# A fused attention and mixture-of-experts kernel: two score tiles of the second head pair issued ahead of the last three products of the first, and the seventh batch's scatters one at a time

## The chip, the cores and the metric

One core of one Trainium2 chip. The metric is device microseconds of one execution of the whole program, measured by repeated runs; the figure that a forecast stands on is the median of the runs. A profile is one further execution, taken with the hardware profiler.

## What is computed

The input is x of 8 batches (B) x 1024 tokens (S) x 512 features (D), float32. Two layers follow each other, each with a layer norm ahead of it and the input added behind it.

```python
# attention layer, 16 heads of 32 features; xh = layernorm(x) cut into heads
theta_q = xh / (1.0 + jnp.abs(w_q)) + b_q + t * phi_q
theta_k = xh / (1.0 + jnp.abs(w_k)) + b_k + t * phi_k
theta_v = xh / (1.0 + jnp.abs(w_v)) + b_v
Q = jnp.concatenate([cos_q, sin_q], axis=-1)      # 64 wide
K = jnp.concatenate([cos_k, sin_k], axis=-1)
...
# mixture of experts: 8 experts, the best 2 for each token, at most 160 rows for each batch and expert
probs = jax.nn.softmax(x @ Wr + br, axis=-1)
topk_p, topk_e = jax.lax.top_k(probs, K)
...
h = jax.nn.relu(jnp.einsum('enc,ech->enh', buf, W1) + b1[:, None, :])
y = jnp.einsum('enh,ehc->enc', h, W2) + b2[:, None, :]
```

Scores are Q K^T with a causal mask and a softmax; the values are cosine plus sine of theta_v, and the attention's output goes through a sine and a cosine once more before the input is added. In the second layer a token's place in the queue of its expert decides whether it is kept.

## The kernel before

**The loop.** The attention is one loop of 32 iterations n, `for n in range(NCK)`. Iteration n is batch b = n // 4 and chunk c = n % 4: four heads, 128 features, all 1024 tokens. The four heads are two pairs (0 and 1). A pair's keys lie as 64 features by 1024 tokens on each half of the partitions, so each step issues two matmuls, one for each head, on half of the array each. Queries are taken in two halves h of 512.

**Scores.** `scores(pair, h, es)` is a generator: each step makes one tile of exponentials. It takes a PSUM tile from `two_banks()` (a pool of three such tiles, shared by everything that uses it), issues the score matmuls (L685), for blocks on the diagonal the mask as further matmuls (L699), and one exponential on ScalarE from PSUM to SBUF (L705). For h = 0 there are three steps (512 queries wide, 512 made of two pieces, 256 wide), for h = 1 seven.

**Products.** `attend(n, pr, h, es, halves)` has the same three or seven steps: a step multiplies one tile of exponentials by the values into one PSUM bank `av` (L719). With the last step of a half goes one instruction on VectorE, which takes the bank to SBUF with a scaling, `av_sb` (L727).

**turn.** `turn(pr, halves, p)` transposes a pair's two `av_sb` tiles into a `two_banks()` tile by 16 transposes on TensorE (L215), the first eight from queries 0 to 511, the last eight from 512 to 1023; VectorE then takes a reciprocal of the softmax sums (L754) and multiplies (L756).

**Order of an iteration.** `some(count, *gens)` steps generators. In iteration n TensorE sees, in this order: scores of pair 0 (with products of the iteration before in between), seven products left from the iteration before (three, four), turn(1) of the iteration before, then the products of pair 0 (three, and after some work on VectorE and ScalarE for the next iteration's keys, the rest), then scores of pair 1, turn(0), the other score tiles, and the first products of pair 1. Between them stand steps of the router of the batch before (`route_on`), in iterations with c = 1 and c = 2: transposes, the logits (L858) and the sums (L875) of a group of tokens, with VectorE's instructions for them. `qk_post` makes the next iteration's queries and keys on VectorE (L450); its second half, `rest(post)`, stands behind turn(0).

**Who decides the order.** For TensorE, VectorE, ScalarE and SyncE the order of the program text is kept, the order is written by hand. Waits come from data and buffer dependencies.

**Scatters.** When the router has placed the 1024 x 2 rows of a batch, 16 indirect DMAs on GpSimd write pairs of token number and gate to `slot_d[b]` in HBM (L770, in `scatter`). They write one tensor, so each waits for the one before, unless `together` is given: then it is declared that their rows are their own, and they are put behind the last weight mixture on GpSimd's queue so far. `fetch_slots(b)` reads the result and waits for all 16. Batches 0 to 5 are scattered within the loop, at c = 3 of the next batch, one at a time. Batch 6 (the seventh) and batch 7 are scattered in `ending()`, together: eight of batch 6 at the first step, the other eight ahead of the router's step "tiles" of batch 7, and batch 7's sixteen at the end.

**The experts.** `ending()` is a generator whose steps are taken inside the first products of the experts: `layer1` (L1189) takes one step for each product. The first chunk's weights are mixed on GpSimd for the first six of its quarters q (`mix_w1`, L1173, four subtractions, into a pool of two buffers), and the scatters of batch 6 stand between these mixtures on GpSimd's queue. Behind `layer1` comes `layer2` (L1234).

The middle of an iteration, where the change lies, and the end of the loop are in the listing.

Of the kernel before, what the change touches and what calls it, by code (L numbers as in the profile page):

```python
# [25 lines left out]
NTT = S // P  # L26
NCH = D // P
HPC = P // DH
E, HID, TOPK = 8, 2048, 2
# [44 lines left out]
def preln_attn_moe_kernel(  # L74
# [133 lines left out]
    def two_banks():  # L208
        return ps_sc.tile([P, 2, 512], F32, name="ps_s")
# [232 lines left out]
    def square(p):  # L442
        f = p.bitcast(U16).rearrange("p (s two) -> p s two", two=2)[:, :, 0]
        nc.scalar.activation(p.bitcast(F32), f, AF.Square, bias=split_c, scale=1.0 / FINE)

    def sine(r):
        nc.scalar.activation(r.bitcast(F32), r, AF.Sin, scale=STEP_ACT)
# [196 lines left out]
    def o_pre(n, pos):  # L644
        c = n % NCH
        p = pos.bitcast(I32)
        r = trig.tile([P, S], I32, name="t_r")
        nc.vector.tensor_tensor(by_token(p), by_token(pos), along(bias_o, c), ALU.add)
        angle(p, r)
        return p, r  # L650

    def o_post(n, st):

        f, s = st[0], st[1].bitcast(F32)
        b, ch = divmod(n, NCH)
        times(s, f, s)
        xt, stats = mid_tiles[b]
        xs = xt[:, :, ch * P : (ch + 1) * P]
        nc.vector.scalar_tensor_tensor(xs, by_token(s), SUM_UNIT, xs, ALU.mult, ALU.add)
        yield  # L660
        for t in range(NTT):
            nc.vector.bn_stats(stats[:, t, ch, :], xt[:, t, ch * P : (ch + 1) * P])


    def tiles_of(h):


        def block(kb, at=0):
            q0 = max(512 * h, kb * P)
            return kb, q0, 512 * (h + 1) - q0, at  # L670

        d = 4 * h
        full = [[block(kb)] for kb in range(d + 1)]
        return full + [[block(d + 1), block(d + 3, 3 * P)], [block(d + 2)]]

    def scores(pair, h, es):

        for parts in tiles_of(h):
            n = sum(w for _, _, w, _ in parts)
            ps = two_banks()  # L680
            own_keys = parts[0][0] >= 4 * h
            for kb, q0, w, at in parts:
                for a in range(2):
                    r = slice(a * 64, (a + 1) * 64)
                    nc.tensor.matmul(  # L685
                        ps[:, a, at : at + w], lhsT=pair[r, 1, kb * P : (kb + 1) * P],
                        rhs=pair[r, 0, q0 : q0 + w], start=at == 0, stop=not own_keys,
                        skip_group_check=True,
                    )
            if own_keys:  # L690

                for part, w in ((0, 64), (1, P)):
                    for a in range(2):
                        r = slice(a * 64, (a + 1) * 64)
                        out_, late = ps[:, a, :w], later_b[r, part, :w]
                        if len(parts) == 2:
                            out_ = ps[:, a, :].rearrange("p (k q) -> p k q", q=P)[:, ::3, :w]
                            late = late.unsqueeze(1).to_broadcast([64, 2, w])
                        nc.tensor.matmul(  # L699
                            out_, lhsT=keys_b[r, part, :], rhs=late,  # L700
                            start=False, stop=part == 1, skip_group_check=True,
                        )

            e = ep.tile([P, 2, n], F32, name=f"e_{n}", bufs=8 if n == 512 else 2)
            nc.scalar.activation(  # L705
                e, ps[:, :, :n], AF.Exp, scale=UNIT * UNIT / math.sqrt(2 * DH)
            )
            es.append(e)
            yield

    def attend(n, pr, h, es, halves):

        vt = v_tiles[n % 2]
        av = ps_av.tile([P, 512], F32, name="av")
        tiles = tiles_of(h)
        for i, parts in enumerate(tiles):
            for kb, q0, w, at in parts:
                for a in range(2):
                    nc.tensor.matmul(  # L719
                        av[a * 64 : (a + 1) * 64, q0 - 512 * h :],  # L720
                        lhsT=vt[:, kb, 2 * pr + a, :], rhs=es[i][:, a, at : at + w],
                        start=kb == 0, stop=i + 1 == len(tiles),
                    )
            if i + 1 == len(tiles):
                av_sb = avp.tile([P, 512], F32, name="av_sb")
                q = 2 * (n % NCH) + pr
                nc.vector.tensor_scalar(av_sb, av, inv_o[:, q : q + 1], None, ALU.mult)  # L727
                halves.append(av_sb)
            yield

    def some(count, *gens):

        for gen in gens:
            while count and next(gen, 0) is None:
                count -= 1
# [7 lines left out]
    def turn(pr, halves, p):  # L743

        ps = two_banks()
        for t in range(NTT):

            by_halves(
                ps[:, :, t * 64 : (t + 1) * 64],
                halves[t // 4][:, t % 4 * P : (t % 4 + 1) * P],  # L750
            )
        av = ps.rearrange("p a (t f) -> p t a f", f=64)
        rec = small.tile([P, NTT, 2, 1], F32, name="rec")
        nc.vector.reciprocal(rec, av[:, :, :, DH : DH + 1])  # L754
        dst = p.rearrange("p (t a d) -> p t a d", a=HPC, d=DH)
        nc.vector.tensor_tensor(  # L756
            dst[:, :, 2 * pr : 2 * pr + 2, :], av[:, :, :, :DH],
            rec.to_broadcast([P, NTT, 2, DH]), ALU.mult,
        )
# [3 lines left out]
    scattered = {b: [] for b in range(B)}  # L763
    mixed = []

    def scatter(count=2 * NTT * TOPK, together=False):

        for _ in range(min(count, len(scatters))):
            b, idx, src = scatters.pop(0)
            queued = nc.gpsimd.indirect_dma_start(  # L770
                out=slot_d[b], out_offset=bass.IndirectOffsetOnAxis(ap=idx, axis=0),
                in_=src, in_offset=None,
            )
            ins = queued.ins
            if together:
                tc.add_manual_dep(
                    ins, mixed[-1].name,
                    mybir.DependencyInfo(
                        mybir.DependencyClass.NoSync, mybir.DependencyReason.DATA
                    ),  # L780
                    reason="behind the mixture",
                )
                for other in scattered[b]:
                    tc.declare_no_dep(ins, other, reason="rows of their own")
            scattered[b].append(ins)
# [506 lines left out]
    def experts_begin():  # L1292
# [6 lines left out]
        mix_w1(0, 0)  # L1299

    def experts(ending):
        pools["hp"] = to_end.pool("hp", NHQ, **right)
        pools["ps_tr"] = to_end.pool("ps_tr", 2, space=PSUM, reuse_waits="tile")
# [67 lines left out]
    for n in range(NCK):  # L1371
        more, late = n + 1 < NCK, last is not None
# [14 lines left out]
        products = [attend(n, 0, h, es[h], halves[0]) for h in range(2)]  # L1387
        if late:
            products.insert(0, attend(n - 1, 1, 1, e11, halves1))
        ahead = [scores(pairs[0], h, es[h]) for h in range(2)]  # L1390
# [8 lines left out]
        def route_on(slot):  # L1399
            if c == slot and route is not None:  # L1400
                next(route)
# [61 lines left out]
        if c == 3 and b > 0:  # L1463
            next(route)
            if b > 1:
                fetch_slots(b - 2)
            if b < B - 1:
                scatter()
# [14 lines left out]
        if more:  # L1483
            post = qk_post(qk_st)
            next(post)
        some(NTT, *products)

        es, halves1 = [[], []], []
        ahead = [scores(pairs[1], h, es[h]) for h in range(2)]
        route_on(1)  # L1490
        route_on(2)
        some(2, *ahead)
        turn(0, halves[0], pos_n)
        next_pairs = rest(post) if more else None
        some(1, *ahead)
# [42 lines left out]
    def ending():  # L1538

        o_st = o_pre(NCK - 1, pos_n)  # L1540
        scatter(NTT * TOPK // 2, together=True)
        yield
        sine(o_st[1])
        square(o_st[0])
        for _ in range(3):
            yield
        for _ in o_post(NCK - 1, o_st):
            yield
        yield
        for name in router(B - 1):  # L1550
            if name == "tiles":
                scatter(together=True)

            for _ in range({"tiles": 5, "places": 5}.get(name, 1)):
                yield
        fetch_slots(B - 2)
        scatter(together=True)
        fetch_slots(B - 1)

    experts(ending())  # L1560

# [30 lines left out]
```

## Time and profile before

| | |
|---|---|
| time, median of 3 runs | 3274.17 us (3273.48 to 3274.39) |
| the profiled execution: its own time | 3271.21 us |
| its span in the profile | 3269.5 us |
| TensorE clock granted, mean | 0.997 of full speed |
| VectorE busy | 2255.6 us, 69% |
| ScalarE busy | 1323.1 us, 40% |
| GpSimd busy | 420.2 us, 13% |
| score matmuls L685, TensorE | 599.5 us in 3072 instructions |
| products L719, TensorE | 524.6 us in 3072 instructions |
| scatters L770, GpSimd | 155.6 us in 128 instructions |
| first product of the experts (L1189) | at 1274.89 us |

The span begins with the first instruction and ends with the last; the execution's own time also has what lies around it (1.7 us here). The execution that was profiled is 3.0 us under the median of the timed runs. Up to about 1275 us the attention loop runs, behind that the experts; an iteration of the loop takes 36 to 42 us. Where a row of the profile ends in brackets, the first number is the idle time of that engine just ahead, in us, and what stands behind the arrow is the work that ended it; "remote" and "issue" name no instruction. A shape such as 64*128 64x512 is that of the weights and of the moving data of a matmul. L numbers are lines of the kernel before.

### The profile page before, as it was taken

To read this page: it belongs to the slowest core of one execution; us is meant where nothing else is said; L and a number is where in the kernel's file an instruction comes from. 1 tells how busy PE (TensorE), PEld (TensorE's weight loads), DVE (VectorE), ACT (ScalarE), POOL (GpSimd) and SP (SyncE) were. 2 spreads that over 40 slices of the span, in tenths; PEclk is the share of its full clock that TensorE was granted. 3 is DMA by queue.
4 is the path that set the end of the run, shared out by engine and by line. 5 is a ranking of instruction groups with operands and counts; after the bars stand their busy time and mean duration, and the time that the engine had idled before them with its cause. 6 is when DMAs were issued, how large, how long until landed. Compare 5 with 4: busy or idle time off the path is not lost.

```text
span 3269.5 us, 48752 instructions
## 1 busy us (share of the span) xinstructions
PE 3188.8 (98%) x18942; PEld 2164.7 (66%) x18942; DVE 2255.6 (69%) x4961; ACT 1323.1 (40%) x1617; POOL 420.2 (13%) x387
## 2 busy tenths in 40 slices
PE   5999999999999998999999999999999999999998
PEld 2444444444444444688688688688688688688687
DVE  8888888878788675755755755755755755855854
ACT  7888887888887874211111111111201201201201
POOL 3000202011120212311011011011011011011010
PEclk9999999999999999999999999999999999999999
DMA  5435454453545352323223223323322322322321
GB/s 163 143 98 164 133 146 143 135 156 104 181 117 159 94 172 56 117 55 85 90 50 81 91 52 77 94 52 71 100 50 73 101 47 73 103 46 71 104 42 26
DMA packets 235254, 319.74 MB, mean 98 GB/s; under 512 B 22456, under 2 KB 155280, under 8 KB 222992
## 3 DMA queue, kind: packets, MB, share of 16 engines
q1 hardware_dynamic: 211664, 273.38, 28.5%
q0 software_dynamic: 22912, 43.22, 7.5%
q8 instruction: 150, 2.46, 0.3%
q14 instruction: 80, 0.66, 0.1%
q10 hardware_dynamic: 448, 0.02, 0.0%
HBM read 187.62 MB, written 61.82 MB: 76 GB/s over the span
## 4 chain that ended last, share of the span: by engine, by line
PE 57%; DVE 0%; DMA 0%; issue 0%; POOL 0%; POOLq 0%; DVEq 0%
PE ps_p L1234 29%; PE ps_p L1189 27%; PE ps_t L1135 1%; DMA out_dram<-y,slots 0%; DMA slots<-slot_d 0%; DVE w_t L1068 0%; DVE w L1067 0%; DVE w_t L1066 0%; DVE w_t L1069 0%; POOL slot_d L770 0%; POOLq L1588 0%; POOL slots L1005 0%; DVE y L1250 0%; DVE p L1271 0%; DVE p L1272 0%
## 5 line engine op out<-in xcount | busy, mean ns | idle before, releaser
L705 ACT ACTIVATE e<-ps_s 128x1024 f32<-128x1024 f32 (+1 forms) x640 | 569.6, 937 | 195.5 <-PE ps_s L685 111.9
L685 PE MATMUL ps_s<-qk 64*128 64x512 f32 (+3 forms) x3072 | 599.5, 506 | 39.4 <-DMA qk<-qk_r 12.4
L1234 PE MATMUL ps_p<-w,hid 128*128 128x256 f32 x2560 | 567.2, 379 | 0.0
L1234 PEld LDWEIGHTS ps_p<-w,hid 128*128 128x128 f32 x2560 | 484.4, 190 | 66.7 <-DVE u L1210 0.3
L719 PE MATMUL av<-e,v 128*64 128x512 f32 (+3 forms) x3072 | 524.6, 491 | 0.6 <-ACT e L705 0.6
L1234 PE MATMUL ps_p<-w_t,hid 128*128 128x256 f32 x1920 | 430.3, 379 | 0.6 <-DVE w_t L1068 0.6
L685 PEld LDWEIGHTS ps_s<-qk 64*128 64x128 f32 x3072 | 262.1, 188 | 228.4 <-issue 106.6
L1234 PEld LDWEIGHTS ps_p<-w_t,hid 128*128 128x128 f32 x1920 | 361.3, 190 | 48.2 <-DVE w_t L1068 1.0
L719 PEld LDWEIGHTS av<-e,v 128*64 128x64 f32 x3072 | 200.5, 137 | 285.7 <-issue 267.7
L1189 PE MATMUL ps_p<-xe,w 128*128 128x256 f32 (+1 forms) x1024 | 297.8, 434 | 1.1 <-issue 1.1
L1189 PE MATMUL ps_p<-xe,t 128*128 128x256 f32 (+1 forms) x1024 | 297.0, 433 | 0.0
L1189 PE MATMUL ps_p<-xe_s,t 128*128 128x256 f32 (+1 forms) x1024 | 296.9, 433 | 0.0
L770 POOL DMA_INDIRECT slot_d<-token,slot x128 | 155.6, 1215 | 975.6 <-issue 621.2
L1265 ACT COPY p<-ps_p 128x256 f32<-128x256 f32 x40 | 14.7, 369 | 604.8 <-PE ps_p L1234 604.8
L1189 PEld LDWEIGHTS ps_p<-xe,t 128*128 128x128 f32 x1024 | 194.3, 190 | 81.2 <-issue 1.0
L1189 PEld LDWEIGHTS ps_p<-xe,w 128*128 128x128 f32 x1024 | 193.4, 190 | 82.1 <-DVE hid L1207 3.7
L1189 PEld LDWEIGHTS ps_p<-xe_s,t 128*128 128x128 f32 x1024 | 194.3, 190 | 80.7 <-issue 0.4
L1094 POOL DMA_INDIRECT xg<-xn_d,source x76 | 74.5, 980 | 1073.6 <-PE ps_t L1135 1064.3
L1256 POOL DMA_INDIRECT out_dram<-y,slots x80 | 126.5, 1581 | 624.3 <-DVE y L1251 624.3
L1204 ACT ACTIVATE p<-ps_p,b_t 128x256 f32<-128x256 f32 (+1 forms) x128 | 65.4, 511 | 335.6 <-PE ps_p L1189 178.4
L1221 ACT ACTIVATE hid<-hid,b_more 128x256 f32<-128x256 f32 (+1 forms) x128 | 71.8, 561 | 278.0 <-DVE hid L1220 270.7
L1208 ACT ACTIVATE hid<-hid 128x256 f32<-128x256 f32 (+1 forms) x128 | 60.1, 470 | 297.9 <-DVE hid L1207 289.8
(224 smaller groups left out, 3822.9 us busy)
## 6 DMA issues: line engine op xcount, KB each, us to landing
w<-in_L_ffn_W_dram SPq DMA_DIRECT2D x256, 256.0 KB
w<-in_L_ffn_W_dram SPq DMA_DIRECT2D x64, 512.0 KB
qk<-qk_c SPq DMA_DIRECT2D x124, 256.0 KB
qk<-qk_r SPq DMA_DIRECT2D x124, 256.0 KB
qk_base<-base_d SPq DMA_DIRECT2D x28, 1024.0 KB
xn_d<-xn SPq DMA_DIRECT2D x72, 256.0 KB
x_mid<-in_L_attn_x_dram SPq DMA_DIRECT2D x16, 1024.0 KB
out_dram<-x_mid SPq DMA_DIRECT2D x8, 2048.0 KB
```

The lines of the kernel that those rows point to most:

```text
L685: nc.tensor.matmul(ps[:, a, at : at + w], lhsT=pair[r, 1, kb * P : (kb + 1) * P], rhs=pair[r, 0, q0 : q0 + w], start=at == 0, stop=not own ...
L705: nc.scalar.activation(e, ps[:, :, :n], AF.Exp, scale=UNIT * UNIT / math.sqrt(2 * DH))
L719: nc.tensor.matmul(av[a * 64 : (a + 1) * 64, q0 - 512 * h :], lhsT=vt[:, kb, 2 * pr + a, :], rhs=es[i][:, a, at : at + w], start=kb == 0, ...
L770: queued = nc.gpsimd.indirect_dma_start(out=slot_d[b], out_offset=bass.IndirectOffsetOnAxis(ap=idx, axis=0), in_=src, in_offset=None,)
L1094: ins = nc.gpsimd.indirect_dma_start(out=xg, out_offset=None, in_=xn2_d[i % 2], in_offset=bass.IndirectOffsetOnAxis(ap=source[:, e, j0 + j ...
L1135: nc.tensor.transpose(ps[:, c, :], xg[:, c * P : (c + 1) * P], ident)
L1189: nc.tensor.matmul(ps, lhsT=weights[:, k, :], rhs=rows[:, k, :], start=k == 0, stop=k == 1)
L1204: nc.scalar.activation(p1, product(b11, a11), AF.Identity, bias=b1_t[:, e * NHC + q : e * NHC + q + 1])
L1208: nc.scalar.activation(h11, h11, AF.Relu)
L1221: nc.scalar.activation(h12, h12, AF.Relu, bias=more)
L1234: nc.tensor.matmul(ps, lhsT=hs[k][:, part, cols], rhs=ws[k][weight], start=k == 0, stop=k == NHQ - 1,)
L1256: ins = nc.gpsimd.indirect_dma_start(out=out, out_offset=bass.IndirectOffsetOnAxis(ap=meta[:, e, jj[r], 0:1], axis=0), in_=ys[r], in_offse ...
```

## The change

Two edits. In the loop, seven products of pair 0 are left at that point, those of half 1. Before, all seven are issued, then the router's steps, then pair 1's score generators are made and stepped twice, which gives the first two score tiles, and then comes turn(0). After, four of the seven are issued, then the two score tiles, then the last three products with their `av_sb`, then the router's steps, and turn(0). Iteration 0 has its products used up before this point, so that there nothing moves.

In `scatter` a third way, `late`: behind the last mixture, like `together`, but each scatter still waits for the one before on the same tensor. `ending()` scatters batch 6 in this way: eight at its first step as before, and the other eight as four and four, at the first and the fourth step of the router of batch 7, in place of eight at its step "tiles". Batch 7's sixteen stay together. In the built program GpSimd's queue thereby holds twelve scatters, the mixture of one quarter, four scatters and the next mixture, where it held eight, a mixture, eight, and a mixture.

```diff
--- before.py
+++ after.py
@@ -763,7 +763,7 @@
     scattered = {b: [] for b in range(B)}
     mixed = []
 
-    def scatter(count=2 * NTT * TOPK, together=False):
+    def scatter(count=2 * NTT * TOPK, together=False, late=False):
 
         for _ in range(min(count, len(scatters))):
             b, idx, src = scatters.pop(0)
@@ -772,7 +772,7 @@
                 in_=src, in_offset=None,
             )
             ins = queued.ins
-            if together:
+            if together or late:
                 tc.add_manual_dep(
                     ins, mixed[-1].name,
                     mybir.DependencyInfo(
@@ -780,6 +780,7 @@
                     ),
                     reason="behind the mixture",
                 )
+            if together:
                 for other in scattered[b]:
                     tc.declare_no_dep(ins, other, reason="rows of their own")
             scattered[b].append(ins)
@@ -1483,13 +1484,14 @@
         if more:
             post = qk_post(qk_st)
             next(post)
-        some(NTT, *products)
+        some(4, *products)
 
         es, halves1 = [[], []], []
         ahead = [scores(pairs[1], h, es[h]) for h in range(2)]
+        some(2, *ahead)
+        some(NTT, *products)
         route_on(1)
         route_on(2)
-        some(2, *ahead)
         turn(0, halves[0], pos_n)
         next_pairs = rest(post) if more else None
         some(1, *ahead)
@@ -1538,7 +1540,7 @@
     def ending():
 
         o_st = o_pre(NCK - 1, pos_n)
-        scatter(NTT * TOPK // 2, together=True)
+        scatter(NTT * TOPK // 2, late=True)
         yield
         sine(o_st[1])
         square(o_st[0])
@@ -1547,9 +1549,12 @@
         for _ in o_post(NCK - 1, o_st):
             yield
         yield
+        steps = 0
         for name in router(B - 1):
-            if name == "tiles":
-                scatter(together=True)
+
+            if steps in (0, 3):
+                scatter(NTT * TOPK // 4, late=True)
+            steps += 1
 
             for _ in range({"tiles": 5, "places": 5}.get(name, 1)):
                 yield
```

## Prediction

> **What bounds the kernel now.** I began with the page's busy times and slices.
>
> ```profile
> PE 3188.8 (98%) x18942; PEld 2164.7 (66%) x18942; DVE 2255.6 (69%) x4961; ACT 1323.1 (40%) x1617; POOL 420.2 (13%) x387
> PE   5999999999999998999999999999999999999998
> ```
>
> TensorE is at 98%, full from the second slice on: an edit counts only by the TensorE time or idling that it adds or takes. So I read the order of time on TensorE in one iteration of the attention loop, n=15 (c=3). Columns: start, us, engine, line, operation.
>
> ```profile
> 624.71 7.96 PE L719 MATMUL av<-e,v 128*64 128x512 f32 x48
> 632.60 1.13 PE L685 MATMUL ps_s<-qk 64*128 64x512 f32 x4
> 634.73 0.66 PE L215 MATMUL ps_s<-ident,av_sb 64*128 64x64 f32 x16
> 635.22 0.66 PE L685 MATMUL ps_s<-qk 64*128 64x256 f32 x4
> 636.01 1.99 PE L685 MATMUL ps_s<-qk 64*128 64x512 f32 x8
> 638.42 2.37 PE L719 MATMUL av<-e,v 128*64 128x512 f32 x16
> 640.73 2.85 PE L685 MATMUL ps_s<-qk 64*128 64x512 f32 x12
> ```
>
> Ten products (L719), two score tiles, the 16 transposes of turn(0), the 256-wide tile, two 512-wide tiles. There is no idle but 0.20 us ahead of 636.01, where the weight load waits for the exponential ("0.20 <-ACT e L705" in the same view). ScalarE and VectorE in that stretch:
>
> ```profile
> 632.39 1.28 ACT L705 ACT_TABLE_LOAD   x1
> 633.85 2.75 ACT L705 ACTIVATE e<-ps_s 128x1024 f32<-128x1024 f32 x3 [0.17 <-PE ps_s L699]
> 632.71 0.75 DVE L727 TENSOR_SCALAR av_sb<-av,inv_o 128x512 f32<-128x512 f32 x1 [0.59 <-PE av L719]
> ```
>
> ScalarE loses 0.17 us to the score tiles; and L727, which makes the `av_sb` that turn(0) reads, runs 632.71 to 633.46 wholly under the two score tiles. The change takes that cover away. One place has the new order already: the end of the loop, products and then a turn.
>
> ```profile
> 1266.64 5.81 PE L719 MATMUL av<-e,v 128*64 128x512 f32 x32
> 1272.38 0.46 PE L215 MATMUL ps_s<-ident,av_sb 64*128 64x64 f32 x8
> 1273.30 0.46 PE L215 MATMUL ps_s<-ident,av_sb 64*128 64x64 f32 x8 [0.46 <-DVE av_sb L727]
> 1272.50 0.75 DVE L727 TENSOR_SCALAR av_sb<-av,inv_o 128x512 f32<-128x512 f32 x1 [9.45 <-PE av L719]
> ```
>
> Eight transposes go at once (queries 0 to 511, ready long before); the other eight wait for L727. Last, the place where scatters are issued together, iteration n=31:
>
> ```profile
> 1247.52 1.13 PE L685 MATMUL ps_s<-qk 64*128 64x512 f32 x4
> 1251.19 0.70 PE L685 MATMUL ps_s<-qk 64*128 64x256 f32 x4 [0.87 <-issue]
> 1252.87 1.13 PE L685 MATMUL ps_s<-qk 64*128 64x512 f32 x4 [0.89 <-ACT e L705]
> 1257.16 1.92 PE L685 MATMUL ps_s<-qk 64*128 64x512 f32 x4 [3.17 <-DVE o_p L756]
> 1262.17 2.85 PE L685 MATMUL ps_s<-qk 64*128 64x512 f32 x12
> 1256.04 0.26 DVE L754 RECIPROCAL rec<-ps_s 128x16 f32<-128x16 f32 x1 [7.64 <-remote]
> 1244.68 0.99 POOL L770 DMA_INDIRECT slot_d<-token,slot  x1 [14.72 <-DVE token L982]
> 1253.57 0.96 POOL L770 DMA_INDIRECT slot_d<-token,slot  x1 [0.30 <-issue]
> POOL slot_d L770 <- DMA slot_d<-token,slot: 234.6, 89, 6.3
> ```
>
> L754 needs only turn(0), whose transposes are recorded from 1249.66 on, yet starts at 1256.04; an exponential due at 1252 starts at 1256.19, also "remote". Completion on TensorE is seen some 4 to 6 us late while GpSimd issues scatters back to back, and until just after. The last line counts the scatters that go one at a time (batches 0 to 5): 89 waits, none beside such a stall.
>
> **The change part by part, on TensorE's time.**
>
> *No instruction is added.* By the built order VectorE, ScalarE and SyncE keep their instructions, order and waits; TensorE changes order, GpSimd order and waits. No DMA is moved past another on SyncE.
>
> *A second block of products, iterations 1 to 30.* Count a product of 512 columns as one unit: the x48 row is 9 units in 7.89 us (624.71 to 632.60), the x16 row 2.5 in 2.31 (638.42 to 640.73). The difference gives 5.58/6.5 = 0.858 us a unit, so 0.165 us for each block as such. Going from a mask into products costs more than into a turn: 609.14 to 609.32 against 624.03 to 624.11, 0.10. Together 0.265 us.
>
> *turn(0) uncovered.* 1272.38 to 1273.30 is 0.92 us for eight transposes; all sixteen take 0.49 at 634.73, so half is 0.25: +0.67. Bounds: the idle alone, 0.46, and the whole of L727 with its 0.12 start, 0.87. I take 0.67, the same pattern. Queued behind on TensorE are the 256 tile and everything after it; on VectorE L754, L756 and the second half of the key post-processing (L450, 2.28 us) go late with it, by no more than TensorE itself.
>
> *What is won.* The scores come 2.3 us sooner, so ScalarE starts right after the table load. TensorE gains what it waited for that: 0.20 a time (bounds 0 and 0.27, 635.22 to 636.01 against 0.52 for the same tile at 623.59).
>
> - c=3 and c=0, n=3, 4, 7, ... 28: 14 times 0.265+0.67-0.20 = 0.735, 10.3 us.
> - c=1, n=5, ... 29: seven times. Now the router's matmuls (L858, L875) stand between products and turn: 557.04 to 557.74, 0.70, and cover the 0.67. 0.07 each, 0.5 us.
> - c=2, n=6, ... 30: seven times. L858 covers 596.36 to 596.72, 0.36: 0.31+0.265-0.20, and about 0.08 because VectorE's four place instructions (597.15 to 598.12) now follow the late L727 and hold the PSUM slot that the next score tile wants. 0.45 each, 3.2 us.
> - n=1, 2: no router, and no wait for ScalarE to win: 0.94 each, 1.9 us. n=0: products are used up before, nothing moves.
>
> Sum: +15.9 us. Bounds: with 0.46 for the wait and 0.27 won, +9; with 0.87 and nothing won, +25.
>
> *Scatters of batch 6 one at a time.* Now eight and eight together (1.26 us apart), then 12 and four, each waiting for the one before. The six series of batches 0 to 5 took 54 to 64 us for 15 steps, 3.9 us a step on the mean, 2.36 at the least. The stall goes: 1247.52 to 1262.17 is 14.65 us; the same stretch in n=15 is 8.13, less 0.59 for transposes that n=31 hasn't, plus this change's 0.735: 8.28. Gain 6.4 us. It includes the half clock after the idle (granted 0.72 in 1256 to 1262; the tile at 1257.16 took 1.85 us for 0.96). Bounds: 0 if the stall has another cause, 7 if the small waits at 1297 to 1302 go too.
>
> *What is queued behind them.* GpSimd's weight mixtures (L1173) for the third and fourth quarter. Twelve from 1244.68 at 3.9 end at 1291.5; the mixture's second part is then ready about 1293. TensorE wants it at 1298.17 now, 1291.8 after the gain: 1 us late at the mean step, nothing at 2.36. The stretch 1244 to 1256 has a DMA share of 0.02 against 0.39 at 476 to 536, so I take a step near 2.4 and no cost. The four others end before 1305, the fourth quarter wants its mixture at 1317.56. Unhidden, each 1 us of step costs 12.
>
> A rule that speaks against it stands in the Trainium skill, "DMA: Bandwidth & Descriptors", section on the SWDGE path: a transfer issued by GpSimd has a fixed cost of about 2 us, mostly the wait for the write to be confirmed, so waiting for each one lays that bare. By an estimate from that page twelve would take 12 x (0.96+2.0) = 35.5 us, and the sum would stay as it is.
>
> **Sum.** 15.9 - 6.4 = +9.5 us. The profiled execution took 3271.21 around a span of 3269.5; its span would be 3279.0. It is 3.0 under the median of the runs, 3274.17, on which the forecast stands: 3283.7 us. Its own range is +4 to +15: 3278 to 3289.
>
> **Rivals.**
>
> 1. *ScalarE paces the iterations, and its head start counts whole: faster.* The place is the first exponential after the table load: idle before it 0.17 at c=3 and c=0, 0.70 at c=1, 0.67 at c=2. If TensorE's later waits for ScalarE took up the 0.94, the gain would be 14 x 0.17 + 7 x 0.70 + 7 x 0.67 = 12.0, with the 6.4 of n=31 18.4: 3255.8. It decides from 0.94 us of later waiting per iteration. For it: ScalarE is at 70 to 80% here. Against: past 636.01 n=15 shows no such wait. 13%.
> 2. *The stall of n=31 stays,* being due to something else: +15.9, 3290.1. For it: "remote" names no cause. Against: the stall comes again beside the next series issued together (1363.50, 2.76 idle at ScalarE's p), never beside single ones. 15%.
> 3. *The serial scatters hold the mixtures up.* At the slowest series' step, 63.5/15 = 4.23, the third quarter is 1295.4+2.4-1291.8 = 6.0 late: +15.5, 3289.7. Against: the empty DMA queues. 8%.
> 4. *Gain and loss cancel:* the wait at its low bound, the gain at its high one: +9-7 = +2, 3276. 10%.
>
> **How the numbers follow.** Main case 54%. A run here tells no change from one under 0.2%, 6.5 us. A seventh of the main case lies under that, with rival 4 that is 17%; faster is rival 1, 13%, and 2% of surprises; slower the rest, 68%. The range 3268 to 3292 leaves out rival 1 and the ends of 2 and 3.
>
> **What would show it.** TensorE in c=3 and c=0: two score tiles inside the products, a turn in two halves of eight with about 0.46 idle for L727 (some 16 times), and no wait at the first 512 tile; no ScalarE idle after the table load. n=31: no "remote" wait, clock 1.00 there. L1189 never waiting for L1173's mixture. I am wrong if turn(0) shows no idle, if L754 in n=31 still starts 6 us late, or if an iteration of c=3 stays at 35.87 us (634.73 to 670.60) instead of 36.6.

## The result and the profile after

In the same series of runs the changed kernel took 3279.11 us (median of nine, 3274.85 to 3283.11) and the kernel before 3273.63 us (median of nine, 3269.91 to 3274.39): 5.5 us slower, a ratio of 1.0018, 95% interval 1.0010 to 1.0027. The forecast was 9.5 us, in a range of its own of +4 to +15. The two profiled executions differ by more, spans of 3279.9 and 3269.5 us, because the one of before was a short one of its kernel and the one of after a long one; the sizes below are therefore taken from single iterations and from medians, not from the two spans.

TensorE in iteration n=15 (c=3) of the changed kernel, the counterpart of the stretch shown for before; columns are start, us, engine, line, operation, and in brackets the idle ahead of it. From here on a line number in a row is that of the run's own kernel (L1190 after is L1189 before):

```profile
634.79 1.13 PE L685 MATMUL ps_s<-qk 64*128 64x512 f32 x4
...
637.02 2.37 PE L719 MATMUL av<-e,v 128*64 128x512 f32 x16
639.33 0.46 PE L215 MATMUL ps_s<-ident,av_sb 64*128 64x64 f32 x8
640.25 0.46 PE L215 MATMUL ps_s<-ident,av_sb 64*128 64x64 f32 x8 [0.46 <-DVE av_sb L727]
640.55 0.65 PE L685 MATMUL ps_s<-qk 64*128 64x256 f32 x4
...
641.12 1.94 PE L685 MATMUL ps_s<-qk 64*128 64x512 f32 x8
```

The turn is split in two halves of eight, and the second waits 0.46 us for `av_sb`. The wait of 0.20 us ahead of the first 512-wide tile, which before had at 636.01, is gone. VectorE and ScalarE in the same stretch:

```profile
639.45 0.75 DVE L727 TENSOR_SCALAR av_sb<-av,inv_o 128x512 f32<-128x512 f32 x1 [2.64 <-PE av L719]
638.04 1.94 ACT L705 ACTIVATE e<-ps_s 128x1024 f32<-128x1024 f32 x2
641.33 0.60 ACT L705 ACTIVATE e<-ps_s 128x512 f32<-128x512 f32 x1 [1.35 <-PE ps_s L215]
```

ScalarE does start its exponentials right after the table load, without the 0.17 us of before, and then stands 1.35 us for TensorE, which is in the turn. The head start is lost at once.

Iteration n=31, where before had TensorE idle for 0.87, 0.89 and 3.17 us; TensorE, VectorE and GpSimd:

```profile
1263.86 0.46 PE L215 MATMUL ps_s<-ident,av_sb 64*128 64x64 f32 x8
1264.78 0.46 PE L215 MATMUL ps_s<-ident,av_sb 64*128 64x64 f32 x8 [0.46 <-DVE av_sb L727]
...
1267.52 2.37 PE L719 MATMUL av<-e,v 128*64 128x512 f32 x16
1265.29 0.26 DVE L754 RECIPROCAL rec<-ps_s 128x16 f32<-128x16 f32 x1 [0.56 <-PE ps_s L215]
1261.05 0.97 POOL L770 DMA_INDIRECT slot_d<-token,slot  x1 [1.42 <-DMA slot_d<-token,slot]
```

The scatters go every 2.4 us or a little more (twelve from 1258.63 to 1287.01, 2.58 us a step), and L754 waits 0.56 us for the transposes, where it waited 7.64. The granted clock from 1255 to 1265 is 1.00, where it was 0.83.

The length of an iteration, from the start of the sixteenth exponential (of twenty) of the iteration before it to that of its own, is worked out from the trace. Means over n=4 to 29 without n=19, which stands by itself; us (the runs below the first two are described under Experiments):

| kernel | c=3 | c=0 | c=1 | c=2 | n=19 | n=31 |
|---|---|---|---|---|---|---|
| before | 35.87 | 35.66 | 43.75 | 37.46 | 35.87 | 45.14 |
| after | 36.59 | 36.14 | 43.82 | 38.01 | 37.96 | 38.83 |
| scores_alone | 36.59 | 36.13 | 43.81 | 38.01 | 37.96 | 45.24 |
| scatters_alone | 35.88 | 35.71 | 43.71 | 37.47 | 35.88 | 39.30 |
| one_tile_behind | 36.17 | 35.86 | 43.88 | 37.76 | 37.23 | 38.48 |
| two_in_flight | 35.88 | 35.68 | 43.58 | 37.47 | 35.87 | 40.91 |
| before_again | 35.88 | 35.59 | 43.73 | 37.47 | 35.87 | 46.57 |
| filled_again | 35.88 | 35.75 | 43.55 | 37.47 | 35.88 | 39.29 |

The iterations n=1 to n=30 together take 1160.56 us in the changed kernel and 1145.42 in before: 15.1 us more. In n=31 it takes 6.3 us less. (Single iterations of before take 35.4 to 44.1 us in these, a little more than the 36 to 42 given at the start.)

The end of the first part of the experts in the changed kernel, TensorE:

```profile
1282.54 4.51 PE L1190 MATMUL ps_p<-xe,w 128*128 128x384 f32 x8 [1.13 <-issue]
...
1370.05 1.56 PE L1190 MATMUL ps_p<-xe,t 128*128 128x384 f32 x4 [3.62 <-issue]
1371.44 1.45 PE L1190 MATMUL ps_p<-xe_s,w 128*128 128x384 f32 x4
1375.18 12.31 PE L1235 MATMUL ps_p<-w,hid 128*128 128x256 f32 x48 [2.28 <-DVE hid L1208]
```

Here batch 7's sixteen scatters are still issued together, and TensorE stands 3.62 and 2.28 us; before had one idle of 2.76 us at this place. The first row took 4.51 us, where before had 2.82 for the same eight products: the granted clock is 0.50 from 1283.12 to 1286.53. Of the 10.4 us between the two profiled spans 8.8 lie in the loop (15.1 - 6.3), 2.8 behind it, and 1.2 go the other way ahead of it. In the 2.8 are the two things seen here, 3.1 us more of idle and 1.7 of clock, and against them shorter waits of TensorE further on, told below.

### The profile page after: what moved, and what is told of

Its sections match the earlier page's. It is cut to its first block, busy times and chain, and to the rows that moved or that the text cites. A ratio compares the mean times of both kernels' runs of the same rounds, so it can differ in the third digit from the quotient of the medians.

```text
span 3279.9 us, 48776 instructions
## 1 busy us (share of the span) xinstructions
PE 3196.8 (97%) x18942; PEld 2162.3 (66%) x18942; DVE 2252.9 (69%) x4961; ACT 1319.0 (40%) x1617; POOL 418.5 (13%) x387
## 4 chain that ended last, share of the span: by engine, by line
PE 74%; DVE 4%; issue 1%; DMA 1%; ACT 1%; SPq 0%; POOLq 0%; DVEq 0%; ACTq 0%
PE ps_p L1235 29%; PE ps_p L1190 28%; PE av L719 7%; PE ps_s L685 7%; PE ps_t L1136 1%; PE ps_s L215 1%; PE ps_s L699 1%; DVE qk_f L526 0%; ACT e L705 0%; DVE qk_r L450 0%; DVE av_sb L727 0%; DMA xn_d<-xn 0%; DMA qk<-qk_r 0%; DVE xT L839 0%; DVE xn L814 0%
## 5 line engine op out<-in xcount | busy, mean ns | idle before, releaser
L1190 PE MATMUL ps_p<-xe,t 128*128 128x256 f32 (+1 forms) x1024 | 297.1, 433 | 3.6 <-issue 3.6
L1190 PE MATMUL ps_p<-xe,w 128*128 128x256 f32 (+1 forms) x1024 | 299.4, 435 | 1.1 <-issue 1.1
L1190 PE MATMUL ps_p<-xe_s,t 128*128 128x256 f32 (+1 forms) x1024 | 296.9, 433 | 0.0
L1190 PEld LDWEIGHTS ps_p<-xe,t 128*128 128x128 f32 x1024 | 194.3, 190 | 84.9 <-issue 4.6
L1190 PEld LDWEIGHTS ps_p<-xe,w 128*128 128x128 f32 x1024 | 194.1, 191 | 82.9 <-DVE hid L1208 3.7
L1190 PEld LDWEIGHTS ps_p<-xe_s,t 128*128 128x128 f32 x1024 | 194.3, 190 | 80.8 <-issue 0.7
```

What stands on the lines that cost most here:

```text
L1190: nc.tensor.matmul(ps, lhsT=weights[:, k, :], rhs=rows[:, k, :], start=k == 0, stop=k == 1)
```

## Experiments

Each series of four ran on a chip of its own, with the kernel before beside it, so that a difference between series can be one of the chip or of the hour. The median of before was 3275.6 us in the first series, 3263.9 in the second and 3274.8 in the third, so a kernel is compared only with before in its own series.

### First series: the parts, and two ways of undoing half of one

**scores_alone.** The new order of scores and products with the old scatters.

```diff
-        some(NTT, *products)
+        some(4, *products)
...
+        some(2, *ahead)
+        some(NTT, *products)
         route_on(1)
         route_on(2)
-        some(2, *ahead)
```

> The new order of score tiles and products alone; the scatters are as in the kernel before. Theory (the products' own block and the uncovered av_sb cost TensorE 0.72 us in an iteration with c=3, 0.55 with c=2): the loop gains 13 to 15 us up to n=30, the stall of n=31 stays (L754 waits over 5 us, TensorE 4 to 5 us idle), total +12 to +16 us, 3286 to 3290. Rival A (the order costs little, and the 10 us between the two profiled executions are mostly luck of the last stage): total +4 to +7. Rival B (ScalarE's head start counts): faster by over 5 us.

Measured: 3291.15 against 3275.61 us, +15.5 (ratio 1.0046, 1.0032 to 1.0060). The loop costs 15.4 us by the trace, and the stall of n=31 stays (n=31 takes 45.24 us). VectorE, then TensorE:

```profile
1266.65 0.75 DVE L727 TENSOR_SCALAR av_sb<-av,inv_o 128x512 f32<-128x512 f32 x1 [6.74 <-remote]
1267.46 0.46 PE L215 MATMUL ps_s<-ident,av_sb 64*128 64x64 f32 x8 [2.23 <-DVE av_sb L727]
1272.12 1.18 PE L685 MATMUL ps_s<-qk 64*128 64x512 f32 x4 [2.71 <-DVE o_p L756]
```

With the new order the wait is split in two: `av_sb`, which has to see the end of the last product, starts late, and TensorE stands 2.23 us for it; L754 then waits 3.59 us, less than the 5 expected. TensorE's 2.23 and 2.71 us of idle are the 4 to 5 expected. The rival of a cheap order falls, and ScalarE's pace with it.

**scatters_alone.** The old order with the new scatters.

```diff
-        scatter(NTT * TOPK // 2, together=True)
+        scatter(NTT * TOPK // 2, late=True)
...
-            if name == "tiles":
-                scatter(together=True)
+            if steps in (0, 3):
+                scatter(NTT * TOPK // 4, late=True)
+            steps += 1
```

> The scatters of batch 6 one at a time as in the changed kernel, with the old order of scores and products. Theory (scatters issued back to back make TensorE's completions late): iteration n=31 is 38.1 us instead of 45.1, first product of the experts near 1268.5, total -4 to -7 us, 3267 to 3270, unless the stall beside batch 7's sixteen scatters grows, which it may by up to 4. Rival (the stall of n=31 has another cause, and went because n=31 came at another time): n=31 keeps a wait of L754 of over 4 us, total -1 to +1.

Measured: 3266.03 against 3275.61 us, -9.6 (0.9969, 0.9959 to 0.9980). The stall of n=31 is gone, more is won than expected, and batch 7's stall stays:

```profile
1249.43 0.26 DVE L754 RECIPROCAL rec<-ps_s 128x16 f32<-128x16 f32 x1 [2.62 <-PE ps_s L215]
1355.49 1.56 PE L1190 MATMUL ps_p<-xe_s,w 128*128 128x384 f32 x4 [3.05 <-ACT p L1205]
```

Most of L754's 2.62 us is the time of the score tiles and transposes that TensorE has ahead of it. The two parts add up: +15.5 - 9.6 = +5.9, against +5.5 for both together.

**one_tile_behind.** The changed kernel with the second score tile behind the last products.

```diff
-        some(2, *ahead)
+        some(1, *ahead)
         some(NTT, *products)
         route_on(1)
         route_on(2)
+        some(1, *ahead)
```

> The changed kernel, but only the first score tile goes ahead of the last three products; the second stands behind them (and behind the router's steps), so that it covers the av_sb instruction of 0.75 us again. Theory (0.67 of the 0.735 us is the uncovered av_sb): no idle of 0.46 us in the turn, iterations with c=3 take 35.9 to 36.0 us instead of 36.59, with c=2 37.4 to 37.7 instead of 38.01, and the total is 9 to 13 us under the changed kernel's 3279.1: 3266 to 3270. Rival (it is the split into two blocks of products, or ScalarE's order, that costs): c=3 stays at 36.4 to 36.6, total 3277 to 3280.

Measured: 3272.51 us, -3.1 against before (0.9992, 0.9983 to 1.0001); c=3 takes 36.17 us, between the two theories. TensorE in n=15:

```profile
632.66 1.13 PE L685 MATMUL ps_s<-qk 64*128 64x512 f32 x4
...
633.80 2.37 PE L719 MATMUL av<-e,v 128*64 128x512 f32 x16
636.11 1.14 PE L685 MATMUL ps_s<-qk 64*128 64x384 f32 x8
...
637.24 0.66 PE L215 MATMUL ps_s<-ident,av_sb 64*128 64x64 f32 x16
```

The turn is whole again, sixteen transposes and no idle. What stays above before, 36.17 - 35.88 = 0.29, is the second block of products; and the wait for ScalarE ahead of the 512-wide tile is back (0.30 us from the mask at 638.22 to 638.52, against 0.08 in the changed kernel). My expectation of 35.9 to 36.0 had kept that gain, which one tile ahead doesn't bring. So in c=3: 0.29 for the block, 0.22 won, and 0.715 - 0.29 + 0.22 = 0.65 for the uncovered turn. The 0.65 is what is left over; read from the rows the turn takes 1.22 us (639.33 to 640.55) for 0.49 before, 0.73 more, so the split between the terms is good to some 0.1 us.

**two_in_flight.** The kernel before, with each scatter of the series issued together waiting for the one two places ahead.

```diff
-                for other in scattered[b]:
+                for other in scattered[b][:-2] + scattered[b][-1:]:
                     tc.declare_no_dep(ins, other, reason="rows of their own")
+                for other in scattered[b][-2:-1]:
+                    tc.add_manual_dep(
...
```

> The kernel before, with one thing added: in the series issued together a scatter waits for the one two places before it, so at most two are on their way, where eight could be. A single one takes 2.4 us from issue to its release, so that two at a time can still be issued every 1.3 us. Theory A (it is the dense issue on GpSimd that makes TensorE's completions late): the stall of n=31 stays, L754 waits over 5 us, total within 2 us of before. Theory B (it is the number of writes on their way): the wait of L754 is under 1.5 us, n=31 takes 38 to 39 us, the stall at batch 7's series is gone too, total -6 to -11 us.

Measured: 3279.50 us, +3.9 (1.0010, 1.0001 to 1.0019), which neither theory had. VectorE, GpSimd and TensorE:

```profile
1253.39 0.26 DVE L754 RECIPROCAL rec<-ps_s 128x16 f32<-128x16 f32 x1 [5.06 <-PE ps_s L685]
1248.95 0.96 POOL L770 DMA_INDIRECT slot_d<-token,slot  x1 [0.79 <-DMA slot_d<-token,slot]
1377.83 0.18 DVE L1093 TENSOR_SCALAR source<-slots 128x32 int32<-128x32 int32 x1 [14.49 <-DMA slots<-slot_d]
1379.33 1.22 PE L1242 MATMUL ps_p<-w_t,hid 128*128 128x256 f32 x2 [10.46 <-DVE w_t L1076]
```

Three of seven gaps between the scatters of n=31 grew from 0.30 to 0.7 or 0.8 us, and the stall shrank (n=31 40.9 us, between 39.3 and 45.1). Batch 7's stall went, but that series now took from 1335.66 to 1371.9 instead of some 20 us, VectorE waited 14.49 us for its slots with the weight mixtures queued behind, and TensorE 10.46 us for those. Dense issue and the number on their way were not told apart: the scatters of n=31 were still 1.46 us apart on the mean, and two at a time left 1.6 us of the stall (40.9 against 39.3).

### Second series: dense issue by itself, and batch 7

**filled.** The kernel before, with an instruction that no output uses behind each of the eight scatters of n=31.

```diff
+            if together and b == B - 2 and len(scattered[b]) <= NTT:
+                tc.keep_in_program_order(
+                    nc.gpsimd.tensor_tensor(spare, spare, spare, ALU.subtract)
+                )
```

> The kernel before, with an ordinary GpSimd instruction of about 1 us (a subtraction on a spare tile) behind each of the eight scatters of batch 6 in n=31. Nothing waits for the write before, up to eight may be on their way, but a scatter is issued every 2.4 to 2.8 us as in the serial series, and GpSimd is never idle. Theory A (the dense issue of scatters makes TensorE's completions late): the wait of L754 falls from 7.6 to under 2.5 us, n=31 takes 38.5 to 40 us instead of 45.1, total -4 to -7 us against before. Theory B (it needs GpSimd waiting, idle, or each write confirmed before the next): L754 still waits over 5 us, n=31 stays over 43, total within 2 us of before.

Measured: 3263.38 against 3263.93 us (1.0001, 0.9991 to 1.0010). That is theory B's total, and n=31 at 39.30 us is theory A's: on this chip it tells nothing. The trace shows why. These are the times at which TensorE's completions are recorded while sixteen scatters of batch 7 are issued back to back, in two kernels that do it alike:

```
rows_late (second series):      1332.92 1334.21 1335.50 1336.79 1338.08 1339.37 1340.66 1341.95 ...
scatters_alone (first series):  1335.57 1336.97 1342.13 1343.42 1354.77 1354.84 1354.90 1354.96 ...
```

On the second chip they come every 1.29 us, as the matmuls end. On the first there is a silence of 11.4 us, and then what was due comes 0.06 us apart, while TensorE's own rows go on ending at most 1.4 us apart: the work is not late, its report is. On the chip of the second series dense scatters hold up no completion.

**last_serial.** scatters_alone with batch 7's scatters one at a time too (`scatter(late=True)` in place of `together=True` at the end of `ending`).

> scatters_alone with batch 7's sixteen scatters one at a time too. Theory: TensorE's 3 us of idle beside that series (3.05 in scatters_alone) goes, but the fetch of the slots (L1006) comes 20 to 45 us later, and VectorE waits for it at L1086 with the mixing of the second layer's weights (L1067 to L1070) queued behind, for which TensorE waits: 8 to 30 us of idle at L1235, total +5 to +28 us against scatters_alone's 3266, 3271 to 3294. Rival (the mixing has lead enough, so that the stall's end counts): total -3 to -6 against it, 3260 to 3263.

Measured: 3287.89 us, +24.0 against before (1.0072, 1.0056 to 1.0087). VectorE, then TensorE:

```profile
1386.16 0.18 DVE L1086 TENSOR_SCALAR source<-slots 128x32 int32<-128x32 int32 x1 [28.89 <-DMA slots<-slot_d]
1387.67 1.22 PE L1235 MATMUL ps_p<-w_t,hid 128*128 128x256 f32 x2 [24.86 <-DVE w_t L1069]
```

As the theory has it: the wait moves to the one instruction on VectorE that needs the slots, and what is queued behind it stops TensorE. This is what issuing together is good for.

**rows_late** and **last_serial_rows_late.** The same two, scatters_alone and last_serial, with that instruction moved behind the mixtures.

```diff
-            if i == 0:
-                find_rows(1)
             rest(mixes)
...
-                aside = behind(2, aside)
+                aside = behind(8, aside)
             for block in range(nh):
+                if i == 0 and block == 1:
+                    find_rows(1)
```

> scatters_alone with the instruction that reads the slots (L1086) moved on VectorE from ahead of the last weight mixtures to the second block of layer2, and the gathers that need it moved with it. Theory: the waits of TensorE for w_t near 1370 (0.72 and 1.01 in scatters_alone's profile) go or shrink, the stall of 3 us beside batch 7's series stays: -1 to -3 us against scatters_alone's 3266, 3263 to 3265. Rival: nothing (within 1 us), since TensorE waits for the mixtures for their own sake.

> rows_late with batch 7's sixteen scatters one at a time. Theory (scatters issued back to back make TensorE's completions late, here too): no idle of 3 us at the end of layer1 (1355 in scatters_alone), none of half clock behind it, and no wait for the slots on TensorE: -4 to -6 us against rows_late, 3258 to 3262; 12 to 16 us under the kernel before. Rival (that idle is the end of layer1 itself, ScalarE's and VectorE's chain behind the last products): the idle of 2.5 to 3 us stays, total as rows_late.

Measured: rows_late 3256.65 us, -7.3 (0.9979, 0.9970 to 0.9988); last_serial_rows_late 3262.85 us, -1.1 (0.9998, 0.9989 to 1.0007). In the first TensorE's waits for w_t remain, 0.91 and 1.01 us, so the mixtures are late for their own sake; how much of the 7.3 us is the move can't be said, since scatters_alone didn't run on this chip. In the second the serial series ends too late even so:

```profile
1393.93 1.08 PE L1136 MATMUL ps_t<-ident,xg 128*128 128x128 f32 x4 [6.10 <-DMA xg<-xn_d,source]
```

There was no stall to win back here.

### Third series: again, where before stalls

**before_again**, the kernel before.

> The kernel before, unchanged, beside the others of this series. In the runs of the last series it took 3263.9 us, against 3273.6 to 3275.6 in the two series ahead of it. Theory (what differs from series to series is whether TensorE's completions come late beside scatters issued densely, and the changed kernel's gain from the scatters is this alone): where the median of before is near 3264, n=31 takes 39 to 40 us and TensorE has no idle of 3 us at the end of layer1; where it is near 3274, n=31 takes 44 to 46 us and the idle is there. Rival (the difference lies elsewhere, spread over the loop): n=31 is 44 to 46 us in any case.

Measured: 3282.27 us in its one execution, in a series whose before has a median of 3274.85. VectorE and TensorE:

```profile
1257.18 0.26 DVE L754 RECIPROCAL rec<-ps_s 128x16 f32<-128x16 f32 x1 [7.81 <-PE ps_s L685]
1258.31 2.08 PE L685 MATMUL ps_s<-qk 64*128 64x512 f32 x4 [2.38 <-DVE o_p L756]
1368.85 1.70 PE L1189 MATMUL ps_p<-xe,t 128*128 128x384 f32 x4 [3.69 <-issue]
```

Both stalls are there, n=31 takes 46.57 us. The half of the expectation on a fast chip could not be tried.

**after_again**, the changed kernel.

> The changed kernel, unchanged. Theory: the new order of scores costs 13 to 16 us everywhere, the scatters win 7 to 10 only where before has its stalls: +4 to +7 us against before where that is near 3274, +11 to +16 where it is near 3264. Rival (the scatters' gain is the same everywhere): +4 to +7 in both.

Measured: 3280.62 us, +5.8 (1.0015, 1.0006 to 1.0024), as in the first comparison. What it does on a chip without the stall wasn't tried.

**filled_again**, as filled.

> filled once more: an ordinary GpSimd instruction behind each of the eight scatters in n=31. Where before has its stall of n=31 in this series: theory A (dense issue is what makes completions late) expects n=31 at 38.5 to 40 us and -4 to -7 us in all, theory B (a confirmed or limited number of writes is what is needed) n=31 over 43 and no gain. Where before has no stall it tells nothing again: within 2 us.

Measured: 3268.16 us, -6.7 (0.9977, 0.9966 to 0.9987). GpSimd and VectorE:

```profile
1247.17 0.99 POOL L772 DMA_INDIRECT slot_d<-token,slot  x1 [0.17 <-issue]
1248.18 1.05 POOL L790 TENSOR_TENSOR spare<-spare 128x512 bf16<-128x512 bf16 x1
1249.40 0.98 POOL L772 DMA_INDIRECT slot_d<-token,slot  x1 [0.17 <-issue]
1250.81 0.26 DVE L754 RECIPROCAL rec<-ps_s 128x16 f32<-128x16 f32 x1 [2.19 <-PE ps_s L215]
```

Of the two theories A holds: GpSimd is scarcely idle (0.17 us) and no write is waited for, only the scatters are 2.23 us apart instead of 1.27; L754 waits 2.19 us, n=31 takes 39.29 us, as with the serial series. In the same execution batch 7's scatters, still dense, leave TensorE's completions silent for up to 6.4 us. So on such a chip spacing alone takes the stall away; neither GpSimd's waiting nor its being idle is needed. One rival is left: the spacing also changes how many writes are on their way. In filled, where the trace has the landings, a write of n=31 landed 2.1 to 2.3 us behind the start of its issue in most cases, just as the next was issued, so that there was about one on its way where the expectation had allowed for eight. Density and number are not told apart by these runs.

**serial_and_pairs.** rows_late with batch 7's series two in flight.

> The version that should beat both: the old order of scores and products; batch 6's scatters one at a time as in the changed kernel; batch 7's with two on their way at most; the slots read on VectorE at the second block of layer2, as in rows_late. Theory: where before has its stalls, n=31 at 39.3 us and no idle of 3 us at the end of layer1: 12 to 18 us under before; where it has none, 4 to 8 us under before. Rival (pairs for batch 7 bring the slots too late even so): TensorE waits for gathered rows or w_t by 5 us or more, and the total is above rows_late's -7.3.

Measured: 3260.16 us, -14.7 against before (0.9959, 0.9946 to 0.9973), and 20.5 under the changed kernel in the same series. TensorE runs into layer2 without a wait (its waits for w_t remain, 0.96 and 1.01 us), and VectorE doesn't wait for the slots:

```profile
1351.84 10.63 PE L1243 MATMUL ps_p<-w,hid 128*128 128x256 f32 x48
...
1380.01 0.17 DVE L1094 TENSOR_SCALAR source<-slots 128x32 int32<-128x32 int32 x1
```

From the first product of the experts (1266.44) to this row it takes 85.4 us, where before took 91.3 and before_again 96.7. What the pairs win and what the later reading of the slots wins was not separated.

## Why the prediction was right, and where it was not

**The sign and the mechanism of the score order: right.** Forecast +15.9 us, measured +15.1 over n=1 to n=30 and +15.5 by scores_alone's median. The total of c=3 holds nearly to the hundredth, 0.735 (0.72), and its terms as far as they can be split: 0.265 for the block (0.29), 0.67 uncovered (0.65 left over, 0.73 from the rows), 0.20 won (0.22). c=1 took the 0.07 forecast; c=2 was forecast at 0.45 and took 0.54; c=0 at 0.735 and took 0.48, since before is sometimes longer there (35.38 to 36.12) where the new order is not; n=1 and 2 took 0.75 and 0.71 of 0.94. One thing was not foreseen: n=19 takes 2.09 us more instead of 0.72, in scores_alone as well. VectorE and TensorE of the changed kernel there:

```profile
771.13 1.23 DVE L440 TENSOR_SCALAR qk_r<-qk_f 128x2048 int32<-128x2048 int32 x1 [3.30 <-DMA qk<-qk_r]
775.54 2.04 PE L685 MATMUL ps_s<-qk 64*128 64x512 f32 x8 [1.11 <-ACT e L705]
```

Before waited 1.70 us for the same transfer, and TensorE not at all. Why it lands later in this one iteration was not tried.

**The stall of n=31: right.** Forecast 6.4 us, measured 6.3. Its cause was put down to scatters issued back to back; filled_again shows that spacing them is enough to end it, with the number on their way as the one rival left.

**The step that failed: the size of the term "Scatters of batch 6 one at a time".** It was put at 6.4 us with an upper bound of 7 "if the small waits at 1297 to 1302 go too"; by scatters_alone it is 9.6 (6.6 to 13.4), whose low end nearly reaches the forecast; that the excess is real rests also on the traces, where the loop alone makes 15.1 - 6.3 = 8.8 us for the 5.5 measured in all. The difference lies, as far as it was found, with the second eight scatters, which stand beside the router's stores of rows (`xn_d`) and the loads of weights. The wait of VectorE there, in before and after:

```profile
1306.43 1.23 DVE L813 TENSOR_SCALAR xn<-x_mid,mv,rstd 128x512 f32<-128x512 f32 x2 [4.27 <-DMA xn_d<-xn]
```

```profile
1313.18 1.85 DVE L814 TENSOR_SCALAR xn<-x_mid,mv,rstd 128x512 f32<-128x512 f32 x2 [2.18 <-DMA xn_d<-xn]
```

It is 4.27, 5.33, 5.19 and 4.99 us in before, before_again, scores_alone and filled_again, which issue these eight together, and 2.18, 2.48, 2.26 and 3.12 in after, scatters_alone, one_tile_behind and after_again, which issue four one at a time. TensorE's waits between the first product and the router's last group (idles over 0.15 us) follow: 3.5, 5.3, 5.4 and 4.9 us against 1.9, 1.6, 1.7 and 3.4, on the mean 2.6 less, though one of the low ones is near one of the high ones. 6.3 + 2.6 is 8.9 of the 9.6.

Two more traces bear on the cause of this part. It doesn't need late completions: filled has it too, 4.62 us on VectorE and 4.7 on TensorE against 2.32 and 1.6 in rows_late, on the chip where completions come in time. And four moved ahead need not be all of it: in two_in_flight all eight begin where they do in before, 11.3 us behind the first product, but are spread over 20 us in place of 9.5, and TensorE's waits are 2.7 us, between the two groups (VectorE waits 2.58 us at the longest, and 2.6 more in three parts). That is one trace; what in the dense eight holds up the stores of `xn_d` was not tried.

With 15.5 - 9.6 the sum is +5.9, which is the result.

**The rivals.** ScalarE's pace fell (1.35 us of new wait at 641.33 in place of the 0.17). That the stall of n=31 stays fell. That the serial scatters hold the mixtures up fell: twelve ended by 1288, and GpSimd's mixture at 1292.30 waited 4.33 us for a buffer that TensorE still read. "Gain and loss cancel" (+2) was about as near to the +5.5 as the main case (+9.5), though for another reason than it gave: the order's cost was not at its low end, the scatters' gain was above its high end.

**The rule weighed against it.** The fixed cost of a GpSimd transfer that the Trainium skill gives in "DMA: Bandwidth & Descriptors", section on the SWDGE path, is about 2 us; the prediction's estimate put it behind the 0.96 of issue. The trace agrees with the 2 us when it is counted from the start of issue, 2.1 to 2.3 us to the landing for six of the eight writes of n=31 in filled. The wait behind issue is shorter than in the estimate, 1.40 to 1.45 us for eight of the eleven waits among the twelve scatters of the changed kernel and 1.87 to 2.07 for the others: the twelve took about 31 us and not 35.5. Beside the loads of weights the wait was up to 7.00 us (rows_late). It decided nothing for batch 6; for batch 7 it is why a serial series ends too late. The six serial series of the loop took 56.1 to 63.5 us, not 54 to 64; nothing rests on the difference.

## What to carry to other kernels

An instruction that only feeds the next stage may be hidden by what happens to stand behind it: before moving work ahead, name what it covers where it stands, here 0.75 us of VectorE under two score tiles, paid for in most iterations (in seven the router's matmuls took over as cover). Small indirect writes issued back to back on GpSimd can be dear to engines that have no part in them; spacing them, by waiting or by putting other work between, is worth trying where a wait ends "remote" or later than its data. But a series made longer needs its reader moved too, with all that is queued behind the reader.

## What was not expected of the hardware

Whether dense scatters make TensorE's completions late differs between the series, and so perhaps between chips: silences of up to 11.4 us in the first series and 11.5 in the third, none in the second, with a series of sixteen that was issued in the same way. Before took 3263.9 us in the second against 3274.8 to 3275.6, and was not profiled there. The missing stall of n=31 is not all of this: filled, which has no such stall in either series, took 3263.4 us in the second and 3268.2 in the third.

Most of the rest lies in n=30, where six indirect gathers (L1094 before) are issued on GpSimd some 1.3 us apart. That iteration takes 36.97 to 36.99 us in all four profiles of the second series, and 39.16 to 41.21 in all ten others, where some completions beside the gathers are recorded 0.06 to 0.09 us apart. So it looks as if dense reads do what dense writes do, with 2.2 us or more to win; no run spaced them, and it is not shown.

The first eight products of the experts stand behind the same idle (0.46 and 1.13 us) in all kernels, and took 2.82 us in seven of the fourteen profiles and 4.51, at half clock, in the other seven: 4.51 in after and 2.82 in after_again. The Trainium skill, "TensorE: Matmul & The Clock Gate", section "The HAM clock gate", has an explanation that fits: activity is judged in windows of 3.4 us that run freely. The traces show such windows. Every stretch of half clock between 1200 and 1500 us lasts 3.41 us or a whole multiple of it, and two in one run start a whole multiple apart: in before at 1257.37 and 1363.18, 31 times 3.413 us. With the windows laid out from there, both idles, 1.59 us, lie in one window in all seven profiles with 4.51, and the products begin at most 0.84 us ahead of its end. In four of the seven with 2.82 a window's edge parts the idles; in the other three they lie in one window, but the products begin 1.00 to 1.36 us ahead of its end. So which way it goes is a matter of where the window's edge falls, and a window with 1.59 us of idle in it can cost 1.7 us.
